# Graph attention on a NeuronCore: the last two node tiles computed from whole adjacency rows instead of gathered neighbour rows

## Chip, cores and metric

The kernel runs on one core of one Trainium2 chip. The metric is the device time of one execution in microseconds (us). Four compute engines matter: TensorE (PE; its weight loads are listed as PEld), VectorE (DVE), ScalarE (ACT) and GpSimd (POOL). SyncE (SP) issues DMAs here, and POOL issues the DMAs that gather or scatter rows by index. POOL in this kernel computes next to nothing: its busy time is the issue of indirect DMAs.

## What is computed

Two graph layers over 4096 nodes of 128 features. The adjacency `adj` is a 4096 x 4096 int32 matrix of zeros and ones, symmetric, with the diagonal set, and about 65 ones in a row. Cut to what matters:

```python
# layer 0: attention with 8 heads over the neighbours
Wh = einsum('nd,hde->hne', x, W);  f1 = Wh . a1;  f2 = Wh . a2      # [8, 4096] each
e = leaky_relu(f1[:, :, None] + f2[:, None, :], 0.2)
att = softmax(where(adj > 0, e, -9e15), axis=-1)
h = elu(einsum('hnm,hmd->hnd', att, Wh))
x = layernorm(x + elu(concat_heads(h) @ W1 + b1)) * gamma + beta
# layer 1: of each node's neighbours every m-th is left out; the rest are sorted
# feature by feature, and the quantiles 0.25, 0.5, 0.75 are averaged
agg = 0.5 * mean_of_quantiles(sorted kept neighbours' x) + 0.5 * x
out = agg @ W.T + b + x
```

Because the attention sums over neighbours first and multiplies by `W` afterwards, a node needs, per head, the weighted sum of its neighbours' x, and only then a product with `W[h]`.

## The kernel before

**Order of the work.** The program has two stages. The first (`gat`, L923) does layer 0 and, mixed into it, builds neighbour lists from the adjacency (`Front`, L302). The second (`sparse`, L1918) gathers, for each of 32 tiles of 128 nodes, the kept neighbours' rows of the new x (`x1_d`) and sorts them on VectorE, with products on TensorE and copies on ScalarE.

**The front.** `Front` reads the adjacency in 32 tiles of 128 rows, grouped into six blocks of 2, 6, 6, 6, 6 and 6 tiles. Each tile's row is read in int32 pieces of 1024 columns (`a_i`, SP's queue), turned to bf16 zeros and ones by ScalarE (`nz`, L380), packed into bit words by TensorE (`ps_words`, L387), and unpacked into lists of node numbers by VectorE (the `MAX8` passes of L191 and L195 among others). Inside a block the 128-row tiles are sorted by degree, so that the last tiles of a block have the longest lists; each node's list, degree and own row go to DRAM as a row of `rows_d`. All this is cut into a list of pieces (`todo`). `advance(n)` runs the next n pieces, and `gat`'s loop calls it between half tiles. What it calls later in the loop is thus what the engines' queues hold later, since each engine takes its instructions in the program's order, apart from priorities set with `issue_after`.

**The table.** `table` (L214) computes, for every node, f1 and f2 of the 8 heads by products with `W·a`, and writes the rows (x, f2, f1) of 144 floats to `xf_d` in DRAM. All neighbour gathers read there.

**The attention loop.** The nodes, in the order of the blocks, make 32 tiles of 128, or 64 half tiles `u` of 64 nodes. A half is four groups of 16 nodes. A partition of a group belongs to one node and one of its eight slots (`SL` = 8). One indirect DMA gathers 128 rows: the next neighbour of each of 16 nodes x 8 slots. So a half needs as many gathers as the sum, over its groups, of a round number: some 30 to 44. Lists are padded with a row that cannot count.

For a half `u` the loop of L1365 and on does this:

- `load(u + 3)` (L1122) issues the gathers of the half three later. They land in `nb` buffers of 18 rows each, of which there are six. A gather waits until the products that used the buffer last are done.
- `rows_sum(u)` multiplies the probabilities with a 0/1 pattern on VectorE (`spread`, L1255), and then TensorE does one f32 128x128 product per gathered set of rows (L1263) into `ps_z`.
- `probabilities(u + 1)` computes the logits and the softmax of the next half on VectorE and ScalarE (L1192 to L1240).
- `collect` (L1278) copies `ps_z` to `zT` on ScalarE.
- Every second tile a generator `combine` is started. One step of it is run per half: products with `W` (L1294), elu, products with `W1`, elu, the layer norm, and an indirect store of the rows of `x1_d` on POOL (L1349).
- `own_row` loads the rows of the tile's own nodes (`me`).

At `u` = 60 the pieces of the front that are left are run, and two POOL gathers fetch the node lists of the first sort tiles. At `u` = 61, behind the last neighbour gather, 24 gathers of x1 rows for the first sort tile are issued (`soon`), which only touch rows of earlier blocks.

The three lines of the neighbour gather's buffers and of its issue, for the names that follow:

```python
rows, used = rowp.tile([P, ROWS, D + H], F32, name="nb"), 0     # 6 buffers, 18 rows each
gather = nc.gpsimd.indirect_dma_start(out=rows[:, used + i, :], in_=xf_d,
    in_offset=bass.IndirectOffsetOnAxis(ap=ids[:, k : k + 1], axis=0))
```

Of the kernel before, what the change touches and what calls it, by code (L numbers as in the profile page):

```python
# [50 lines left out]
P = 128  # L51
# [57 lines left out]

ROWS = 18  # L110
# [103 lines left out]
def table(tc, nc, c, x, w, a1, a2, xf_d, between):  # L214
# [3 lines left out]
    with tc.tile_pool(name="ta", bufs=1) as tp, tc.tile_pool(  # L218
# [33 lines left out]
        for i in range(4):  # L252
            nc.gpsimd.dma_start(
                out=xf_d[1 + i * 1024 : 1 + (i + 1) * 1024, :].rearrange(
                    "(t p) d -> p t d", p=P
                ),
                in_=xf[:, ts(i, 8), :],
            )
# [664 lines left out]
def gat(  # L923
    tc, nc, c, x, adj, xf_d, meta_d, flag_d, w, a1, a2, w1, b1, gamma, beta, x1_d, order, infos, soon
# [26 lines left out]
    with ExitStack() as ctx:  # L951
# [15 lines left out]
        table(tc, nc, c, x, w, a1, a2, xf_d, lambda: advance(2))  # L967
# [56 lines left out]
        def fetch(t):  # L1024
# [34 lines left out]
            info = tp.tile([P, max(BLOCKS), 2], I32, name="info")  # L1059
# [7 lines left out]
        def indices(t):  # L1067

            b = block[t]
            if t in index:  # L1070
                return
            fetch(t)
            ids, first, tops, info, others, ends = fetched[b]
            t0 = START[b]
            for i, (of, k) in enumerate(ends):
                if of == t - t0:
                    to = ids[:, k : k + 1]
                    nc.vector.tensor_tensor(to, to, others[:, i : i + 1], op=ALU.max)
            index[t] = ids, first[t - t0], tops[t - t0], info[:, t - t0, :]
# [3 lines left out]
        def own_row(t):  # L1083
            indices(t)
            if t % TWO == 0:
                me = tp.tile([P, TWO, XF], F32, name="me", bufs=5)
                for j in range(TWO):
                    mes[t + j] = me
# [194 lines left out]
        def combine(t, zT):  # L1283
# [7 lines left out]
            def product(h0):  # L1291
                ps_h = bank().rearrange("p (k n) -> p k n", n=n)
                for k in range(TWO):
                    nc.tensor.matmul(  # L1294
                        ps_h[:, k, :], w_sb[:, h0 + k, :], zT[:, h0 + k, :], start=True, stop=True
                    )
                return ps_h

            pending = []
            for h0 in range(0, H, TWO):  # L1300
                if len(pending) == 2:
                    yield
                    for h, ps_h in pending:
                        elu(nc, zT[:, h : h + TWO, :], ps_h)
# [3 lines left out]
            for h, ps_h in pending:  # L1308
                elu(nc, zT[:, h : h + TWO, :], ps_h)
            ps_y = bank()[:, :n]  # L1310
            for h in range(H):
                nc.tensor.matmul(ps_y, w1_sb[:, h, :], zT[:, h, :], start=h == 0, stop=h == H - 1)
# [47 lines left out]

        stored, ahead = [], []
# [6 lines left out]
        for u in range(2 * NT):  # L1368
            t, half = divmod(u, 2)
            if not half and t + 1 < NT:  # L1370
# [3 lines left out]
            with tc.issue_after(spread):  # L1374
                if u < 2 * START[1]:
                    advance((4, 2, 1, 1)[u])
                elif u < 2 * NT - 4:
                    advance(2 if u in (5, 8) else 1)
# [3 lines left out]
            if u + 3 < 2 * NT:  # L1382
                fetch((u + 3) // 2)
            if u + 1 < 2 * NT:
# [4 lines left out]
            if u + 4 == 2 * NT:  # L1389
# [11 lines left out]
            elif u + 3 < 2 * NT:  # L1401
                held[u + 3] = load(u + 3, after=spread)
            elif u + 3 == 2 * NT:
                with tc.issue_after(gathers[2 * NT - 1][HALF - 1, 0]):
# [10 lines left out]
            with ExitStack() as after:  # L1415
                for ins in behind:
                    after.enter_context(tc.issue_after(ins))
                if u % (2 * TWO) == 0:
                    zT = tp.tile([P, H, TWO * P], F32, name="zT")
                collect(u, ps_z, zT)  # L1420
                for stages in going:
                    next(stages, None)
            if u % (2 * TWO) == 2 * TWO - 1:
                going = going[-1:] + [combine(t - 1, zT)]
# [1089 lines left out]
def gnn(tc, x, adj, w, a1, a2, w1, b1, gamma, beta, lw, lb, out):  # L2514
    nc = tc.nc
    with ExitStack() as ctx:
        dram = ctx.enter_context(tc.tile_pool(name="dram", bufs=1, space=DRAM))
        xf_d = dram.tile([N + 1, XF], F32, name="xf_d")
        x1_d = dram.tile([N + len(PADS), D], F32, name="x1_d")
# [14 lines left out]
            tc, nc, c, x, adj, xf_d, meta_d, flag_d, w, a1, a2, w1, b1, gamma, beta, x1_d,  # L2534
# [43 lines left out]
```

## Time and profile before

| what | value |
|---|---|
| three runs | 8006.99, 8009.91, 8018.21 us; median 8009.91 |
| the profiled execution | 8032.08 us, its span 8030.2 us |
| DVE busy | 5547.1 us, 69% of the span |
| POOL busy | 4358.4 us, 54% |
| ACT busy | 2090.6 us, 26% |
| PE busy, PEld busy | 1431.1 us, 18%; 1107.7 us, 14% |
| DMA | 386.08 MB, 48 GB/s over the span |
| first neighbour gather, last one | 84.6 us, 3424.5 us |
| last store of x1 rows | 3494.5 us |

The page gives busy time by engine, then the span in 40 slices of 201 us with a digit for the busy tenths of each engine, and the costliest groups of instructions. Of its slices these four rows show the two stages:

```profile
PE   4344333333423323310000000000000000000000
...
DVE  4534433433433422258998989999999998997998
...
POOL 5466666656666656665464456545554453454310
PEclk5656655666665656655555555555555555555555
```

The attention stage is the first 17 slices, in which no engine is above six tenths; the sorting stage follows, with VectorE at eight or nine tenths. PEclk is the clock that TensorE was granted, in tenths of full speed. The two groups of indirect gathers are

```profile
L1947 POOL DMA_INDIRECT rows<-x_d,info x2054 | 2054.9, 1000 | 1923.0 <-ACT picked L2047 1304.9
L1122 POOL DMA_INDIRECT nb<-xf_d,ids x2191 | 2105.2, 961 | 1125.2 <-issue 635.0
```

The columns are the line, engine and operation, what it writes and reads, the count, then the busy time and the mean ns of one, then the idle time of the engine just before them and what ended most of it. The first is the sorting stage's, the second the attention's. The last four halves, `u` = 60 to 63, have 36, 37, 39 and 44 gathers.

### The profile page before, as it was taken

The numbers are of one execution on the slowest core, as the hardware profiler recorded it, in microseconds if no ns is written. First come the engines' busy times: TensorE is split into PE (matmuls) and PEld (weight loads), VectorE is DVE, ScalarE is ACT, GpSimd is POOL, SyncE is SP. The second block draws the span as 40 slices with busy tenths as digits, with TensorE's granted clock in tenths as the row PEclk, the third lists the DMA queues.
The fourth block names the chain that finished last, engine by engine and source line by source line (L and its number), as shares of the span: only waits on it lengthen the run. The fifth ranks groups of instructions, "written<-read, shape, count | busy, mean of one in ns | idle before, by whom it ended". The sixth has DMA issues, their size and how long they took to land. (4 is left out here: it accounts for less than half of the span.)

```text
span 8030.2 us, 30780 instructions
## 1 busy us (share of the span) xinstructions
PE 1431.1 (18%) x6349; PEld 1107.7 (14%) x6349; DVE 5547.1 (69%) x8168; ACT 2090.6 (26%) x2423; POOL 4358.4 (54%) x4462
## 2 busy tenths in 40 slices
PE   4344333333423323310000000000000000000000
PEld 2223222322322323310000000000000000000000
DVE  4534433433433422258998989999999998997998
ACT  2111100011000000023343334344443443343333
POOL 5466666656666656665464456545554453454310
PEclk5656655666665656655555555555555555555555
DMA  6432322322322212211111111111111111111100
GB/s 179 93 91 68 76 66 70 69 75 62 57 49 50 57 44 50 49 43 37 29 38 30 31 32 38 36 33 35 36 36 31 33 36 26 30 37 32 26 9 1
DMA packets 279691, 386.08 MB, mean 48 GB/s; under 512 B 189891, under 2 KB 190020, under 8 KB 279476
## 3 DMA queue, kind: packets, MB, share of 16 engines
q0 software_dynamic: 144336, 309.02, 15.9%
q1 hardware_dynamic: 135156, 75.00, 3.6%
q14 instruction: 147, 1.20, 0.1%
q8 instruction: 52, 0.85, 0.0%
HBM read 371.07 MB, written 13.04 MB: 48 GB/s over the span
## 5 line engine op out<-in xcount | busy, mean ns | idle before, releaser
L1992 DVE TENSOR_TENSOR rows<-low,rows 128x1024 f32<-128x1024 f32 (+7 forms) x2118 | 3430.0, 1666 | 248.8 <-ACT low L1985 170.3
L1947 POOL DMA_INDIRECT rows<-x_d,info x2054 | 2054.9, 1000 | 1923.0 <-ACT picked L2047 1304.9
L1122 POOL DMA_INDIRECT nb<-xf_d,ids x2191 | 2105.2, 961 | 1125.2 <-issue 635.0
L1985 ACT COPY low<-rows 128x1024 f32<-128x1024 f32 (+8 forms) x1059 | 1451.9, 1377 | 2110.5 <-DVE rows L1992 1589.4
L1263 PE MATMUL ps_z<-spread,nb 128*128 128x128 f32 x4498 | 801.3, 331 | 1052.6 <-issue 903.7
L1255 DVE TENSOR_TENSOR spread<-e,ps_small 128x1152 f32<-128x1152 f32 (+4 forms) x310 | 338.2, 1115 | 839.0 <-remote 649.7
L1263 PEld LDWEIGHTS ps_z<-spread,nb 128*128 128x128 f32 x4498 | 734.9, 243 | 1131.3 <-issue 999.5
L2054 PE MATMUL low<-sixth_i,picked 128*128 128x128 f32 x300 | 73.0, 425 | 4169.1 <-ACT low L1985 2331.6
L2054 PEld LDWEIGHTS low<-sixth_i,picked 128*128 128x128 f32 x300 | 64.0, 318 | 4178.1 <-ACT low L1985 2336.9
L1992 DVE TENSOR_TENSOR rows<-low_s,rows 128x512 f32<-128x512 f32 (+3 forms) x1056 | 534.2, 540 | 38.9 <-remote 16.0
L1237 ACT ACTIVATE ps_e<-ps_e 128x288 f32<-128x288 f32 (+4 forms) x64 | 24.9, 389 | 2011.2 <-DVE ps_e L1231 1369.8
L1985 ACT COPY low_s<-rows 128x512 f32<-128x512 f32 (+3 forms) x528 | 247.5, 503 | 340.9 <-DVE rows L1992 214.9
L380 ACT ACTIVATE nz<-a_i 128x1024 bf16<-128x1024 int32 x128 | 134.5, 1051 | 673.8 <-remote 266.4
L387 PE MATMUL ps_words<-nz,pows 128*128 128x256 bf16 (+1 forms) x544 | 239.4, 612 | 56.4 <-issue 41.4
L2094 POOL DMA_INDIRECT out<-o,info x32 | 32.0, 1000 | 392.0 <-ACT o L2090 360.1
L1294 PE MATMUL ps_h<-zT,w_ga 128*128 128x256 f32 x256 | 115.3, 613 | 447.2 <-DVE s L1602 208.3
L195 DVE SCALAR_TENSOR_TENSOR key<-key,k 128x256 f32<-128x256 f32 x320 | 151.6, 480 | 44.9 <-remote 10.3
L191 DVE MAX8 k<-key 128x8 f32<-128x256 f32 x352 | 145.0, 420 | 41.7 <-issue 8.1
L1142 DVE TENSOR_TENSOR mine<-me,group 128x64 f32<-128x64 f32 x32 | 6.9, 216 | 223.5 <-remote 144.4
L1192 DVE TENSOR_REDUCE den<-ps_e 128x32 f32<-128x288 f32 (+13 forms) x92 | 31.1, 357 | 187.8 <-ACT ps_e L1237 169.2
L1996 DVE TENSOR_TENSOR rows<-rows 128x256 f32<-128x256 f32 (+7 forms) x259 | 146.9, 574 | 0.0
L1998 DVE TENSOR_TENSOR rows<-rows 128x128 f32<-128x128 f32 (+6 forms) x244 | 142.1, 590 | 3.1 <-remote 2.1
(277 smaller groups left out, 1959.5 us busy)
## 6 DMA issues: line engine op xcount, KB each, us to landing
a_i<-in_adj SPq DMA_DIRECT2D x128, 512.0 KB
nb<-xf_d,ids POOLq DMA_INDIRECT x2191
rows<-x_d,info POOLq DMA_INDIRECT x2054
xf_d<-xf POOLq DMA_DIRECT2D x4, 576.0 KB
soon<-xf_d SPq DMA_DIRECT2D x32, 72.0 KB
me<-rows_d SPq DMA_DIRECT2D x32, 72.0 KB
xf<-in_x POOLq DMA_DIRECT2D x4, 512.0 KB
meta_d<-ids_a SPq DMA_DIRECT2D x5, 324.0 KB
```

Source lines behind the costliest of these rows:

```text
L191: nc.vector.max(out=top, in_=work)
L195: nc.vector.scalar_tensor_tensor(work, work, top[:, 7:8], work, op0=ALU.is_lt, op1=ALU.mult)
L387: nc.tensor.matmul(ps_w[:, :m, ts(i, 2 * part)], self.pows[:, b, :], bits[:, :m, :, b], start=b == 0, stop=b == WBITS - 1,)
L1122: gather = nc.gpsimd.indirect_dma_start(out=rows[:, used + i, :], out_offset=None, in_=xf_d, in_offset=bass.IndirectOffsetOnAxis(ap=ids[:, ...
L1255: last = nc.vector.tensor_tensor(spread[:, :m], e[:, at : at + m, :].unsqueeze(2).to_broadcast(shape), own.unsqueeze(1).unsqueeze(3).to_br ...
L1263: product = nc.tensor.matmul(ps_z[:, g, :], rows[:, k, :D], spread[:, i].rearrange("p j h -> p (j h)"), start=i0 + i == 0, stop=i0 + i == ...
L1947: return nc.gpsimd.indirect_dma_start(out=row, out_offset=None, in_=x1_d, in_offset=bass.IndirectOffsetOnAxis(ap=info[:, col : col + 1], a ...
L1985: nc.scalar.copy(packed, lows)
L1992: done = nc.vector.tensor_tensor(to, packed, highs, op=op)
L1996: nc.vector.tensor_tensor(lows, lows, highs, op=ALU.min)
L1998: nc.vector.tensor_tensor(highs, lows, highs, op=ALU.max)
L2054: product = nc.tensor.matmul(made["ps"], v, to, start=i == 0, stop=i == len(found))
```

## The change

The last two tiles (30 and 31; `LISTED` = 30) leave the loop of halves, which now runs to 60 halves instead of 64. Their attention is computed by a new generator `full()` from the whole rows of the adjacency:

- `table` also writes f2 of all nodes, head by head, to DRAM (`f2_d`, 8 x 4096), by two transposes and two POOL DMAs.
- `full()` first loads x whole, as 32 chunks of 128 nodes (24 into the buffer `soon`, 8 into an `a_i` buffer of the front).
- For each of the two tiles, two indirect DMAs on POOL gather the adjacency rows of its 128 nodes, 2048 columns each, into the front's two `nz` buffers, and VectorE turns them into bf16 masks of 0 and a large negative number, kept in two `a_i` buffers.
- For each head of 8: f2 of all nodes is read to every partition in two DMAs of 1 MB (SP's queue) into the same two `nz` buffers. VectorE adds the mask and takes the maximum in one pass; ScalarE adds f1; VectorE does the leaky relu; ScalarE the exponential, with the sum of a row. That is for two halves of 2048 columns each.
- The probabilities, 128 nodes x 4096, are transposed on TensorE by 32 products with a diagonal matrix that also divides by the sum. ScalarE copies them from PSUM four at a time (into the front's `lists` buffer), and 32 products with the chunks of x accumulate z for the head.
- When all is there, the same `combine` is run for the pair, with `zT` in four buffers of the front.

It uses the front's buffers, and so can begin only when the front's pieces are done. The loop therefore takes two pieces of the front instead of one at every third half from 15 on, so that `todo` is empty after half 41 instead of 50. From then on three steps of `full()` are run per half, behind `collect` and `combine`. There are 34 steps up to the last head's (one for each tile and two for each of its heads), and then `combine`'s. What is left of them at `u` = 57 is run there, ahead of the 24 gathers of `soon`, which moved behind `collect` and which need that buffer. `info` gets three buffers.

The core of the diff:

```diff
+FULLS = 2
+LISTED = NT - FULLS
...
+        f2 = tp.tile([P, H, NT], F32, name="f2_ta")
+        nc.scalar.copy(f2, xf[:, :, D : D + H].rearrange("p t h -> p h t"))
...
+        transpose_all(nc, psum, rows, parts, c["idf"])
+        for i in range(2):
+            nc.gpsimd.dma_start(
+                out=f2_d[ts(i, half), :].rearrange("h (t p) -> (h t) p", p=P),
+                in_=rows[:, ts(i, P)],
             )
...
-                if of == t - t0:
+                if of == t - t0 and t < LISTED:
...
+        def full():
...
+            def wide(dtype):
+                v = fr.tp.tile([P, 2, 2 * quarter], BF, name="nz", bufs=2)
+                return v.rearrange("p m c -> p (m c)").bitcast(dtype)
+
+            for j in range(FULLS):
+                t = LISTED + j
+                own_row(t)
...
+                for q in range(2):
+                    a = wide(I32)
+                    nc.gpsimd.indirect_dma_start(
+                        out=a,
+                        out_offset=None,
+                        in_=adj.rearrange("n (q c) -> (n q) c", q=2),
+                        in_offset=bass.IndirectOffsetOnAxis(ap=rows[:, q : q + 1], axis=0),
+                    )
+                    m = fr.tp.tile([P, quarter], I32, name="a_i", bufs=3).bitcast(BF)
+                    nc.vector.tensor_scalar(m, a, 0.0, -BIG, op0=ALU.is_le, op1=ALU.mult)
+                    masked.append(m)
...
+                yield
+                for h in range(H):
+                    p, tops = [], tp.tile([P, 6], F32, name="tops_f")
+                    for q in range(2):
+                        v = wide(F32)
+                        nc.sync.dma_start(
+                            out=v, in_=f2_d[h, ts(q, N // 2)].partition_broadcast(P)
+                        )
+                        nc.vector.tensor_tensor_reduce(
+                            out=v,
+                            in0=masked[q],
+                            in1=v,
...
+                            op0=ALU.add,
+                            op1=ALU.max,
+                            accum_out=tops[:, q : q + 1],
+                        )
+                        p.append(v)
...
+                    for v in p:
+                        nc.scalar.activation(v, v, AF.Identity, bias=f1, scale=1.0)
+                        nc.vector.scalar_tensor_tensor(v, v, 0.2, v, op0=ALU.mult, op1=ALU.max)
+                    for q, v in enumerate(p):
+                        nc.scalar.activation(
+                            v, v, AF.Exp, bias=less, scale=1.0, accum_out=sums[:, q : q + 1]
+                        )
...
+                    diag = fr.tp.tile([P, NG1], F32, name="key")[:, :P]
+                    nc.vector.tensor_scalar(diag, c["idf"], most, None, op0=ALU.mult)
+                    yield
+                    z = fr.small[:, ts(h % 2, P)]
+                    for k in range(NT // 4):
+                        ps = fr.psum_w.tile([P, 2, NG1], F32, name="ps_words")
+                        ps = ps.rearrange("p m c -> p (m c)")
+                        for i in range(4):
+                            col = (4 * k + i) % (NT // 2)
+                            nc.tensor.matmul(
+                                ps[:, ts(i, P)],
+                                p[(4 * k + i) // (NT // 2)][:, ts(col, P)],
+                                diag,
+                                start=True,
+                                stop=True,
+                            )
+                        pT = fr.tp.tile([P, max(BLOCKS), C1], F32, name="lists")
+                        pT = pT.rearrange("p t c -> p (t c)")[:, : 4 * P]
+                        nc.scalar.copy(pT, ps)
+                        for i in range(4):
+                            m = 4 * k + i
+                            chunk = xs[:, m, :] if m < NT * 3 // 4 else rest[:, m - NT * 3 // 4, :]
+                            nc.tensor.matmul(
+                                z, chunk, pT[:, ts(i, P)], start=m == 0, stop=m == NT - 1
+                            )
+                    nc.scalar.copy(zT(h - h % TWO)[:, h % TWO, ts(j, P)], z)
+                    yield
+            for _ in combine(LISTED, zT):
+                yield
...
-        for u in range(2 * NT):
+        halves_of = 2 * LISTED
+        rest = None
+        for u in range(halves_of):
...
-                elif u < 2 * NT - 4:
-                    advance(2 if u in (5, 8) else 1)
+                elif todo:
+                    advance(2 if u in (5, 8) or u > 12 and u % 3 == 0 else 1)
...
+            if u + 3 == halves_of:
+                for _ in rest:
+                    pass
+                with tc.issue_after(gathers[halves_of - 1][HALF - 1, 0]):
                     for i in range(HIGH[0] - SOON):
...
+            if rest is None and not todo:
+                rest = full()
+            for _ in range(3 if rest is not None else 0):
+                next(rest, None)
+        for _ in rest:
+            pass
```

## The prediction

> **What bounds the kernel now.** I read the busy table by stage first, then GpSimd's (POOL's) timeline in the attention stage, then what its gathers wait for, then TensorE and VectorE beside them. By stage (stretch, its length, then busy us and count of PE, PEld, DVE, ACT, POOL; granted clock, DMA share, GB/s):
>
> ```profile
> 3000.00:3250.00 250.00, 82.02 (x384) 69.41 (x384) 60.52 (x159) 15.08 (x29) 165.15 (x175) 0.60 0.21 49
> 4000.00:5000.00 1000.00, 35.75 (x128) 29.21 (x128) 924.07 (x897) 390.78 (x418) 544.97 (x516) 0.50 0.13 34
> ```
>
> The first is attention (84 to 3495 us), the second the second layer's sorting. Sorting is VectorE's, at 92%; the change does not touch it. In attention POOL is the fullest, at 66%, and that understates it, as its timeline shows:
>
> ```profile
> 3190.49 0.94 POOL L1122 DMA_INDIRECT nb<-xf_d,ids  x1 [0.30 <-issue]
> 3191.74 0.94 POOL L1122 DMA_INDIRECT nb<-xf_d,ids  x1 [0.30 <-issue]
> 3199.27 0.94 POOL L1122 DMA_INDIRECT nb<-xf_d,ids  x1 [6.58 <-PE ps_z L1263]
> 3200.51 0.94 POOL L1122 DMA_INDIRECT nb<-xf_d,ids  x1 [0.30 <-issue]
> ...
> 3424.47 0.94 POOL L1122 DMA_INDIRECT nb<-xf_d,ids  x1 [0.30 <-issue]
> ```
>
> A gather costs 0.94 us and 0.30 before the next: one per 1.25 us. About once per half tile POOL stops, because a row buffer is not free yet. Over the 2191 gathers, the idle time before them:
>
> ```profile
>   issue: 635.0, 2082
>   PE ps_z L1263: 253.3, 23
>   remote: 216.0, 43
> ```
>
> So the stage is 2191 x 1.25 = 2740 us of issue and some 470 us of stops for the products of `rows_sum`, three halves back. Those products are late for a reason that this change meets head on:
>
> ```profile
> 2410.39 0.37 PE L1263 MATMUL ps_z<-spread,nb 128*128 128x128 f32 x1 [2.43 <-issue]
> 2410.40 0.21 DVE L1160 STREAM_TRANSPOSE den_t<-den 128x32 f32<-128x32 f32 x1 [1.64 <-remote]
> 2411.79 0.29 PEld L1263 LDWEIGHTS ps_z<-spread,nb 128*128 128x128 f32 x1 [2.51 <-issue]
> 2412.49 0.37 PE L1263 MATMUL ps_z<-spread,nb 128*128 128x128 f32 x1 [1.73 <-issue]
> 2412.50 0.19 DVE L1164 TENSOR_REDUCE den_b<-den_t 128x4 f32<-128x32 f32 x1 [0.91 <-issue]
> ...
> 2429.99 1.23 PE L1263 MATMUL ps_z<-spread,nb 128*128 128x128 f32 x5 [1.03 <-issue]
> ```
>
> I call this the crawl: TensorE and VectorE each take about one instruction per 1.4 us, on one common beat, waiting for nothing that is shown. Setting its 408 slow products against POOL's timeline, they lie some 17 us or more into an unbroken run of gathers, or within 7 us after it; at 2424 POOL stops and by 2430 the products run at full speed again. Halves with short runs (products at 2300 to 2309 and 2363 to 2372) have none.
>
> **The change, part by part.** The profiled execution's span is 8030 us, 8032 with what lies around it, 22 us over the median of the runs, 8010; differences are worked out inside the profile and put on 8010.
>
> *Removed.* Halves 60 to 63 with 36 + 37 + 39 + 44 = 156 gathers. On POOL they fill 3199.3 to 3425.4, 226 us with their stops. The two node-list gathers (1.25 each) and two of the four stores (1.3 each) inside stay: -221. What follows the last gather (store at 3494.5, 70 us on) is the same chain for half 59: nothing.
>
> *f2 rows at the start.* Two more POOL DMAs behind the four `xf_d` stores (3.61 us together), a copy and two transposes (four take 1.09 us, their copy 0.59). POOL then idles 10.64 us before `w_ga`, waiting for DVE: hidden. Without that cover 5 us.
>
> *Front pieces sooner.* The same 50-odd pieces, now two at every third half from 13 on, so that the front ends at half 41, not 50. The sum of DVE work is unchanged. Halves in which a heavy piece delays DVE show stops of 19 to 31 us (before 1006.6, 1150.4, 1638.0, 2875.8); two in one half may make one stop longer and spare another. I take 0, bounds -30 and +30.
>
> *Two tiles from full rows.* Three steps per half from half 41; 16 heads (8 per tile) at two steps each, 1.5 heads per half, over 10.7 halves. Per head, from the nearest rows:
>
> ```profile
> L1992 DVE TENSOR_TENSOR rows<-low,rows 128x2048 f32<-128x2048 f32 x654 | 1469.7, 2280 | 65.7 <-ACT low L1985 58.0 <-issue 4.3
> L1985 ACT COPY low<-rows 128x2048 f32<-128x2048 f32 x327 | 610.1, 1869 | 733.7 <-DVE rows L1992 595.8 <-issue 127.3 <-DMA rows<-x_d,info 9.4
> L1278 ACT COPY zT<-ps_z 128x512 f32<-128x512 f32 x64 | 37.7, 589 | 284.0 <-remote 158.9 <-PE ps_z L1263 119.3 <-issue 5.8
> ```
>
> - DVE: four passes of 2048, 4 x 2.28 = 9.1, and seven small ones at 0.2: 10.5 us.
> - ACT: four of 2048, 4 x 1.87 = 7.5, eight copies of 512, 4.7, one of 128: 12.4 us.
> - PE: 32 products with the diagonal and 32 with x, all f32 128x128. Such a product shows as two records, and 62 records took 8.99 us: 128 x 0.145 = 18.6 us. The bf16 products of L387 took 0.243 us each at 10 to 40 us, where the granted clock was 0.88, and 0.466 in attention; by that ratio a busier PE would need 9.7. I take 18, since waits for ACT break it up.
> - DMA: two reads of 1 MB. The core moved 272 GB/s at 10 to 40 us and 178 at 40 to 80: 3.9 to 5.9 us each, with about 2 to land: 8.
>
> None is over 47 us per half at 1.5 heads (PE 28 + 10 for `rows_sum`, DVE 16 + some 20). But both halves of a row live in the two `nz` buffers, and the next head's f2 can land there only after TensorE has read them. So heads are serial: products to the last read 16, DMA 8, masked maximum 2.3, ACT 1.9, leaky 2.3, exp 1.9, scale and handoffs 1.5: 34 us. In the built order of VectorE the next head's first maximum stands ahead of `spread` of every second half, and a whole head between a half's last softmax instruction (L1240 of before) and it. What queues behind that wait is `spread`, behind it `rows_sum`, behind it the row buffers, and so POOL. Three heads then pace two halves: 3 x 34 = 102 and some 10 of `spread` and products that nothing covers, 56 us per half. Before, halves 41 to 53 took (2912 - 2252) / 13 = 50.8.
>
> Next the crawl. POOL's runs stay 28 to 44 gathers long, 35 to 55 us, so some 20 to 30 us of each half fall under it, and a head has 256 PE records where a half of `rows_sum` had 140. At about one per 1.2 us it all but stands there. The loss per half lies between 0 (PE would have waited for f2 or DVE anyway, as it does for half of a head) and 28 (it always needs PE); I take 19, nearer the upper end, because freed buffers start POOL just when the next head's products come.
>
> VectorE's long passes may slow gathers: beside two-input passes at 2030.71 one took 1.97 us instead of 0.95. With 64 passes that is at most 64 us of issue, most of it in POOL's own stops: I take 0. The Trainium skill speaks against the change here: "GPSIMD Engine Reference", section "Key points", has POOL share its SBUF interfaces with VectorE, with contention for instructions that have two SBUF inputs. All 64 passes have two; by the rule the 64 us would stand, by the row only part.
>
> Adjacency rows: four POOL DMAs and two maskings of 2.3 per tile, x into `soon`: about 15 us that the first head of each tile waits, bounds 5 and 30.
>
> *Sum.* A half of 56 + 19 = 75 is 24 over before, x 10.7 = +258; -221 + 258 + 15 = +52: 8062, rounded up to 8070 for the two combine steps that come on top. The change breaks even at 70 us per half.
>
> **Rivals.**
> - *Heads serial, crawl not felt* (PE waits for f2 while POOL runs): 56 to 68 per half, -221 + 15 + 56..184, so 7860 to 7988; about 7890. For it: crawl spares long ACT and DVE instructions. Against: it strikes every engine but POOL in the trace.
> - *POOL still paces*: at the clock of 0.88 the head's products take 9.7, the chain 26, two halves 88, under POOL's 2 x 47. Then only 221 less 5 to 20: 7800. The Trainium skill's "TensorE: Matmul & The Clock Gate", section "What's actually happening", says the array is throttled by default and sustained activity releases it; the trace agrees with 0.50 idle and 0.88 busy. By that rule this rival would gain weight, by the attention rows (0.60) not.
> - *Slower by far*: crawl takes 28 and f2 reads share the DMA engines (now 0.25 busy) with gathers, 90 or more per half from half 41 on: -221 + 30 + 420 = 8240. It decides above 70.
>
> **How the numbers follow.** Forecast (70 to 88 per half) 0.48, 8000 to 8200; crawl not felt 0.29; POOL paces 0.13; slower by far 0.10. The likeliest gives 8070, with its own range 8010 to 8200. The range, 7830 to 8230, takes in "crawl not felt" whole; it leaves out "POOL still paces" (0.13) and the far end of "slower by far" (some 0.07), 2 in 10 together. Within 0.2% of 8010 (16 us, what a measurement can tell) lies a thin slice of the first two: 0.06. Faster 0.38, slower 0.56.
>
> **What would show it.** 2035 gathers and their end near 3250 to 3300 if I am right, below 3230 if the gain holds; halves from 41 on of about 75 us against 48 before 41 and after 54; POOL stops of 20 us and more there, ended by PE; f32 products of the heads at one per 1.4 us while POOL runs. The sorting stage should last the same 4530 us. Products at full speed beside long gather runs would refute the crawl, and halves near 48 the serial heads.

## The result, and the profile after

The changed kernel took 8216.28 us (median of 4 runs, 8213.94 to 8236.33) against 8013.65 (4 runs): a ratio of 1.0259, interval 1.0241 to 1.0277. It is slower, as forecast, but by 203 us, where the forecast of 8070 stood for 60 over its 8010. The time is inside the stated range, but outside the forecast's own (8010 to 8200).

The attention stage is 212 us longer in the profiled execution. Where they come from is found by counting POOL's neighbour gathers off in both traces (a half has 28 to 44) and taking the start of each half's first gather:

| stretch | before, us | after, us | difference |
|---|---|---|---|
| to the start of half 44 (no head's products yet) | 2382.3 | 2423.7 | +41.4 |
| halves 44 to 55 (the heads' halves) | 624.1 | 999.4 | +375.3 |
| halves 56 to 59 (of after, to the end of the last gather) | 192.9 | 194.2 | +1.3 |
| halves 60 to 63, to the end of the last gather | 226.1 | none | -226.1 |
| end of the last gather to the last store of x1 | 69.1 | 89.5 | +20.4 |

The sum is +212.3. The sorting stage that follows lasted 4509.5 us against 4535.7. Part of the 41.4 may be chance: in `after_again` and `after_b`, two more traces of the changed kernel on other chips, half 44 begins at 2401.6 and at 2447.7 us. Halves 44 to 55 take 83.3 us in the mean in the changed kernel, and 83.2 and 84.2 in those two. The two stretches that the prediction shows of the kernel before, in the busy table by stage of the changed kernel (same columns):

```profile
3000.00:3250.00 250.00, 120.22 (x804) 114.67 (x804) 75.46 (x130) 62.92 (x79) 80.72 (x84) 0.71 0.21 63
4000.00:5000.00 1000.00, 39.69 (x153) 32.96 (x151) 910.97 (x905) 386.29 (x420) 530.11 (x505) 0.51 0.13 33
```

In attention POOL's busy time has halved, from 165 to 81 us in 250: it isn't issuing more slowly, it is standing still. What its gathers waited for, from the source view of the gather's line (L1141 now, L1122 before):

```profile
  PE ps_z L1282: 656.7, 31
  issue: 590.0, 1934
  remote: 141.8, 28
```

The stops for the products of `rows_sum` rose from 253 to 657 us. "issue", in which POOL waited for nothing that the profile shows, fell with the number of gathers. So the row buffers come free later, because TensorE gets to `rows_sum` later. Why it does is in the timeline of ScalarE and TensorE, first for a head (number 5 of tile 30, counted from 0) whose products lie under a run of gathers:

```profile
2760.40 1.16 PE L1491 MATMUL ps_small<-lists,soon 128*128 128x128 f32 x8 [0.79 <-issue]
2766.82 0.59 ACT L1487 COPY lists<-ps_words 128x512 f32<-128x512 f32 x1 [6.47 <-remote]
2767.46 2.08 PE L1491 MATMUL ps_small<-lists,soon 128*128 128x128 f32 x8 [5.90 <-issue]
...
2769.76 3.19 PE L1478 MATMUL ps_words<-key,nz 128*128 128x128 f32 x14
...
2800.53 0.59 ACT L1487 COPY lists<-ps_words 128x512 f32<-128x512 f32 x1 [33.12 <-remote]
```

and for the next head, whose products fall in POOL's stop of 2794.6 to 2853.3:

```profile
2831.85 1.87 PEld L1478 LDWEIGHTS ps_words<-key,nz 128*128 128x128 f32 x16
2833.11 0.59 ACT L1487 COPY lists<-ps_words 128x512 f32<-128x512 f32 x1 [2.20 <-PE ps_words L1478]
...
2836.78 0.59 ACT L1487 COPY lists<-ps_words 128x512 f32<-128x512 f32 x1 [2.20 <-PE ps_words L1478]
2837.67 0.59 ACT L1487 COPY lists<-ps_words 128x512 f32<-128x512 f32 x1 [0.31 <-PE ps_words L1478]
...
2843.80 0.27 ACT L1494 COPY k<-ps_small 128x128 f32<-128x128 f32 x1 [1.25 <-PE ps_small L1491]
```

In the second, a copy follows its transposing products within a microsecond of their end. In the first, the products of the line before it are through by 2773, and the copy that needs them begins at 2800.5, six microseconds after POOL's last gather of the run, with "remote" as the reason: a wait that the profile can name no releaser for. That is what the prediction called the crawl, in the form it takes in a head. From its first product to its last copy a head took 19 to 22 us in POOL's stops (5 of 16 heads, one of them only in part) and 28 to 83 under gathers; heads were 31 to 32 us apart where one lay in a stop, and 52 to 102 otherwise (61.5 in the mean of all).

### The profile page after: what moved, and what is told of

Its sections match the earlier page's. It is cut to its first block, busy times and chain, and to the rows that moved or that the text cites. A ratio compares the mean times of both kernels' runs of the same rounds, so it can differ in the third digit from the quotient of the medians.

```text
span 8216.3 us, 34499 instructions
## 1 busy us (share of the span) xinstructions
PE 1638.4 (20%) x8077; PEld 1316.3 (16%) x8077; DVE 5657.7 (69%) x8266; ACT 2294.0 (28%) x2657; POOL 4259.0 (52%) x4312
## 5 line engine op out<-in xcount | busy, mean ns | idle before, releaser
L1141 POOL DMA_INDIRECT nb<-xf_d,ids x2035 | 1997.0, 981 | 1409.1 <-PE ps_z L1282 656.7
L1282 PE MATMUL ps_z<-spread,nb 128*128 128x128 f32 x4180 | 709.9, 326 | 811.8 <-issue 592.7
L1274 DVE TENSOR_TENSOR spread<-e,ps_small 128x1024 f32<-128x1024 f32 (+4 forms) x284 | 313.7, 1129 | 718.0 <-remote 551.7
L1282 PEld LDWEIGHTS ps_z<-spread,nb 128*128 128x128 f32 x4180 | 656.7, 238 | 876.2 <-issue 727.6
L1441 DVE CUSTOM_DVE_ANT_0 nz<-a_i,nz 128x2048 f32<-128x2048 bf16 x32 | 73.3, 2289 | 422.5 <-DMA nz<-f_d 295.2
L1487 ACT COPY lists<-ps_words 128x512 f32<-128x512 f32 x128 | 73.9, 585 | 552.7 <-remote 393.2
L1491 PE MATMUL ps_small<-lists,soon 128*128 128x128 f32 x768 | 133.1, 336 | 325.2 <-ACT lists L1487 226.4
L1478 PE MATMUL ps_words<-key,nz 128*128 128x128 f32 x1024 | 157.0, 315 | 116.5 <-DVE key L1470 67.8
L1491 PEld LDWEIGHTS ps_small<-lists,soon 128*128 128x128 f32 x768 | 120.3, 242 | 334.2 <-ACT lists L1487 231.3
L1478 PEld LDWEIGHTS ps_words<-key,nz 128*128 128x128 f32 x1024 | 149.0, 229 | 120.5 <-ACT nz L1464 69.8
```

Of the source, the lines that this page charges most:

```text
L1274: last = nc.vector.tensor_tensor(spread[:, :m], e[:, at : at + m, :].unsqueeze(2).to_broadcast(shape), own.unsqueeze(1).unsqueeze(3).to_br ...
L1282: product = nc.tensor.matmul(ps_z[:, g, :], rows[:, k, :D], spread[:, i].rearrange("p j h -> p (j h)"), start=i0 + i == 0, stop=i0 + i == ...
L1478: nc.tensor.matmul(ps[:, ts(i, P)], p[(4 * k + i) // (NT // 2)][:, ts(col, P)], diag, start=True, stop=True,)
L1491: nc.tensor.matmul(z, chunk, pT[:, ts(i, P)], start=m == 0, stop=m == NT - 1)
```

## The experiments

The runs fell on several chips, and these are of two kinds. On three (and in the runs of the result) the kernel before takes 8013 to 8051 us, on two 7302 to 7304. The crawl is seen on the first kind alone, called chips with the crawl from here on. Each ratio is against the kernel before on the same chip.

| kernel | before there | ratio | interval |
|---|---|---|---|
| pace_only | 7304 | 1.0006 | 0.9997 to 1.0016 |
| pace_again | 8026 | 0.9986 | 0.9967 to 1.0004 |
| heads_alone | 7304 | 1.0382 | 1.0361 to 1.0402 |
| few_products | 7304 | 0.9883 | 0.9863 to 0.9903 |
| few_again | 8051 | 0.9857 | 0.9842 to 0.9873 |
| pauses12 | 7304 | 0.9987 | 0.9978 to 0.9997 |
| after_again (unaltered) | 8017 | 1.0230 | 1.0215 to 1.0245 |
| after_b (unaltered) | 8051 | 1.0288 | 1.0273 to 1.0303 |
| two_steps | 8017 | 1.0173 | 1.0158 to 1.0189 |
| one_head | 8017 | 1.0167 | 1.0150 to 1.0185 |
| paused | 8051 | 1.0149 | 1.0134 to 1.0165 |
| paused_one | 8051 | 1.0082 | 1.0067 to 1.0098 |
| split | 8026 | 1.0384 | 1.0345 to 1.0422 |
| bf16 | 8026 | 1.0060 | 1.0040 to 1.0081 |
| bf16_two | 8026 | 1.0044 | 1.0023 to 1.0065 |
| bf16_paused | 7302 | 1.0162 | 1.0146 to 1.0179 |
| bf16_two_paused | 7302 | 1.0115 | 1.0098 to 1.0132 |
| bf16_two_paused_b | 8047 | 0.9965 | 0.9950 to 0.9979 |

**The front's pace, and one kernel on two kinds of chip.** `pace_only` and `pace_again` are one kernel: no tile from full rows.

```diff
-FULLS = 2
+FULLS = 0
...
-            if rest is None and not todo:
-                rest = full()
...
```

> All 32 tiles come from gathered rows again; only the front's pieces keep the changed kernel's pace (two at every third half), and f2 is still written. In the changed kernel halves 0 to 43 ended 41 us later than before, although no head had begun before half 43. If the sooner front itself costs that, this kernel lies some 41 us over the kernel before, less what halves 42 to 50 save since they have no pieces left (up to 30): 8020 to 8055. If I was right to cost it at nothing: within 30 us of 8013, and no more than 10 from it if pieces only move.

> All 32 tiles from gathered rows, the front's pieces at the changed kernel's pace, as in pace_only, but wanted on a chip with the crawl, where the changed kernel's halves 0 to 43 (with no head yet) ended 41 us late. If the sooner pieces cost that by themselves: ratio 1.002 to 1.005 (41 us less what halves 42 to 50 save). If they only move work: 0.999 to 1.001. Without the crawl 1.0006 was measured.

On neither chip does the pace cost anything that can be measured. With the crawl the halves run 39.8 us behind the kernel before at half 44, much as in the changed kernel (41.4), and 11 behind at half 60. That looks like time spent early and given back, but the trace of the kernel before is of another session, and the changed kernel's own traces differ by 46 us at this point. The pair shows the two kinds of chip at one program. The groups of the gathers and of `rows_sum`'s products on the page without the crawl:

```profile
L1141 POOL DMA_INDIRECT nb<-xf_d,ids x2191 | 2111.4, 964 | 679.5 <-issue 643.1
L1282 PE MATMUL ps_z<-spread,nb 128*128 128x128 f32 x4498 | 576.6, 295 | 189.0 <-DVE spread L1274 188.9
L2133 DVE TENSOR_TENSOR rows<-low,rows 128x1024 f32<-128x1024 f32 (+7 forms) x2118 | 3437.7, 1675 | 68.3 <-ACT low L2126 43.1
```

and with it:

```profile
L1141 POOL DMA_INDIRECT nb<-xf_d,ids x2191 | 2104.2, 960 | 1138.2 <-issue 620.5
L1282 PE MATMUL ps_z<-spread,nb 128*128 128x128 f32 x4498 | 802.7, 332 | 1092.5 <-issue 848.5
L2133 DVE TENSOR_TENSOR rows<-low,rows 128x1024 f32<-128x1024 f32 (+7 forms) x2118 | 3428.6, 1664 | 228.3 <-ACT low L2126 125.3
```

The gathers and VectorE's passes take as long on both. What differs is idle time: TensorE's "issue", 848 us where the other page has 188.9 of 189.0 us as waits for `spread`, POOL's stops (5.9 us for products there against 268), and the hand-overs of the sort. In the trace without the crawl POOL's runs are hundreds of us long, and not one of the 4498 product records of `rows_sum` has more than 0.7 us of idle time before it that the profile names no releaser for; with the crawl 415 have. So all that the prediction called the crawl was seen on one kind of chip only. Each chip served one session (one of them two, 27 minutes apart), so whether the crawl belongs to the chip or to its state at the time isn't shown.

**The heads without gathers beside them.** No step of `full()` runs in the loop; all are run where the drain stands.

```diff
-            for _ in range(3 if rest is not None else 0):
+            for _ in range(0 if rest is not None else 0):
```

> No step of the heads runs in the loop of halves; all 16 run one after the other when the row gathers have been issued up to the last buffers, so POOL is silent beside them. Theory 'turns' (a head is 31 us long when POOL is silent, and every longer head of the changed kernel is longer only because its instructions fall under a run of gathers): heads 31 us apart, 16 x 31 + 20 = 516 us in all; gathers end near 3240, the last x1 store some 3240 + 516 = 3760, total 8260 to 8300. Rival 'long heads' (the 61.5 us per head of the changed kernel are the heads' own chain of reads, passes and products): 16 x 61.5 = 984 us, total near 8740.

This ran on a chip without the crawl. Heads are 31 us apart: 14 of the 15 spacings lie between 28.2 and 32.7, and the first head of tile 31, with its adjacency rows, is 43 behind its predecessor. With the crawl, too, heads are 31 to 32 us apart where one lies in a stop of POOL's. So the serial chain is 31 us, and what is over that in the changed kernel isn't the heads' own. The ratio shows what 16 x 31 us cost when nothing hides them.

**The unaltered kernel elsewhere, and fewer heads per half.** `two_steps` and `one_head`:

```diff
-            for _ in range(3 if rest is not None else 0):
+            for _ in range(2 if rest is not None else 0):
...
-                    advance(2 if u in (5, 8) or u > 12 and u % 3 == 0 else 1)
+                    advance(2 if u in (5, 8) or u > 12 and u % 2 == 0 else 1)
```

(the second hunk in `one_head` alone)

> The changed kernel itself, unaltered, beside the kernel before on the chip that these four kernels share. The four kernels run so far were on a chip where the kernel before takes 7304 us, not 8013; in their traces no instruction crawls and POOL never stops for a product outside the heads' halves. If the crawl under long gather runs is what made the change cost 203 us, then on a chip without it the changed kernel is near the kernel before: halves with heads take some 56 us (3 x 34 + 10 over two), about 15 more than POOL's 41 there, so -203 + 12 x 15 + 25 for the start of each tile: 7270 to 7330. If the heads' length alone did it, it is slower by some 200 there too: 7500. On a chip with the crawl: 8205 to 8235 against 8005 to 8020.

> The changed kernel unaltered once more, beside the three that follow, to tell what chip they share. On a chip where instructions crawl under long gather runs (kernel before near 8015): ratio 1.022 to 1.027. On one where they don't (kernel before near 7304): near 7285, ratio 0.995 to 1.000, by the kernel with the one-column copies, which differs by 39 copies of 0.35 us.

> Two steps of the heads per half instead of three, so one head per half from half 41 on, and what is left of them at half 57 behind the loads of the last half. Without the crawl: a head of 31 us lies in a half of 42 to 58 us of gathers beside 12 us of sums, so POOL paces again but for its slower gathers under VectorE's passes (some 2 us per head) and the heads left over (2 to 3 heads, 31 us each, at the end): 7304 - 203 + 16 x 3 + 80 = 7230. With the crawl: each head still takes its 31 us from POOL, only in other places: 8200 to 8260, no better than three steps. 'Long heads' (61 us each whatever POOL does): a half of 73 us, 17 of them, on either chip no gain over three steps.

> As two_steps, and the front takes two pieces at every second half from 14 on instead of every third, so that the heads begin some three halves sooner and are through before half 57. Without the crawl: no heads left over at the end, 7304 - 203 + 16 x 3 + 10 = 7160. With the crawl: the pieces in earlier halves cost what they cost, 8190 to 8260.

All four ran on chips with the crawl. With one head per half, halves 45 to 49 take 69 to 80 us and the heads are 52 to 104 apart (but for the last of `two_steps`, 36): each still takes 20 us and more from POOL. The gain over three steps is 0.6%, and an earlier start adds nothing that can be told from none (the intervals overlap).

**POOL's pauses.** `pauses12` was meant as a pause on POOL, by one copy of a column behind every 12th gather. It was none: POOL went on 0.35 us later, so on its chip it is the changed kernel with 39 small copies. (In this edit and the next the constants are written out.)

```diff
                     gathers[u][g, i] = gather.ins
+                    since[0] += 1
+                    if 44 <= u < 58 and since[0] % 12 == 0:
+                        nc.gpsimd.tensor_copy(landed, rows[:, used + i, :1])
```

> The changed kernel, with a copy of one column on POOL after every 12th row gather in halves 44 to 57, which waits until that gather has landed; nothing else. 'Turns', with a crawl that only begins 15 to 25 us into an unbroken run of gathers: runs of 12 gathers are 15 us, each pause some 3 us, so no product crawls, POOL needs 34 x 1.25 + 3 x 3 = 52 us per half, heads and sums 1.5 x 31 + 12 = 58, and a half takes 60 instead of 82: 8215 - 12 x 22 = 7950. If a pause of 3 us doesn't end the crawl: halves of 85 to 90 and 8250 to 8310. 'Long heads': pauses only add time, 8215 to 8330, with heads still 50 to 100 us apart.

It tells what the change is worth without the crawl: nothing to speak of, 7294 us against 7304. Halves 44 to 48 take 55.3, 51.7, 54.0, 56.0 and 58.8 us, and POOL paces them: of these 276 us it stopped 4.6 for the products of `rows_sum` (the source view of the gather's line, from 2053.5 to 2329.3 us):

```profile
  issue: 47.3, 162
  PE ps_z L1287: 4.6, 2
```

The halves are longer than the 44 us of `pace_only` because gathers are slower: 49 in the whole run, beside VectorE's long passes for the heads, took 1.6 to 3.1 us, against 0.94 for most. Halves 49 to 52 are another matter. They take 67.4, 110.9, 65.3 and 64.2 us, and POOL stops 86 us in them for products. They follow the start of tile 31, whose adjacency rows are gathered by POOL behind the neighbour gathers in its queue; VectorE stands until they land, and `spread` stands behind VectorE's pass. Without the crawl and in the changed kernel:

```profile
2370.11 1.23 DVE L1430 TENSOR_SCALAR a_i<-nz 128x2048 bf16<-128x2048 int32 x1 [38.32 <-DMA nz<-in_adj,rows_f]
2901.95 1.23 DVE L1425 TENSOR_SCALAR a_i<-nz 128x2048 bf16<-128x2048 int32 x1 [37.87 <-DMA nz<-in_adj,rows_f]
```

Without the crawl heads are mostly 30 to 40 us apart, and their copies never wait for "remote". This is the source view of that copy's line, on the chip without the crawl:

```profile
  PE ps_words L1483: 169.5, 109
  PE ps_small L1496: 27.6, 2
```

and of the same copy in the changed kernel:

```profile
  remote: 393.2, 23
  PE ps_words L1478: 147.6, 76
  issue: 11.8, 6
```

`paused` makes real pauses, `paused_one` adds them to `one_head` (from half 40, behind every 14th gather):

```diff
+                    if 44 <= u < 58 and since[0] % 12 == 0:
+                        for _ in range(16):
+                            held_back.append(
+                                nc.gpsimd.tensor_copy(idle, rows[:, used + i, :1]).ins
+                            )
```

(and the next gather is issued behind the last copy)

> The changed kernel with 16 copies of one column on POOL behind every 12th gather of halves 44 to 57, nothing else: POOL issues no gather for some 5.6 us. With the crawl, if it is a backlog that a run of gathers builds up in 15 to 25 us and that needs 5 to 7 us to drain: no run is longer than 15 us, no product crawls, POOL needs 47 + 3 x 5.6 = 64 us per half and the heads and sums 58, a half takes 66 instead of 82: 8000. If pauses of 5.6 us don't help: 64 + what the heads take from POOL, 85 to 100 per half: 8230 to 8400. Without the crawl POOL's pauses alone count: 41 + 17 = 58 to 62 per half against 55 to 65: 7300 to 7350.

> One head per half and the front faster, as in one_head, with the pauses behind every 14th gather from half 40 on. With the crawl, if pauses end it: POOL 47 + 2.4 x 5.6 = 60 per half instead of 70 over 16 halves: 8147 - 160 = 7990. If they don't: 8230 and over. Without the crawl: POOL paces with its pauses, 41 + 13 = 55 per half over 17 halves: 7280 to 7320.

Taking time from POOL made the kernel faster, by 116 us against the unaltered kernel on that chip, and from 1.0167 to 1.0082 against `one_head`, each on its own chip. A pause on the timeline of `paused`, and then, from the source view, the waits of its heads' copies:

```profile
2550.89 3.85 POOL L1157 COPY idle<-nb 128x1 f32<-128x1 f32 x16 [1.64 <-DMA nb<-xf_d,ids]
```

```profile
  PE ps_words L1489: 170.6, 77
  remote: 103.7, 19
  issue: 41.6, 7
```

With runs of 12 gathers "remote" falls from 396 us in the unaltered kernel on that chip to 104, POOL's stops for products from 696 to 337, and a head's products and copies from 28 to 83 us to 19 to 34, but for one of 70. That shows the cause on such a chip: POOL's gathers slow the heads. Whether it is the length of a run or the number of gathers per us isn't told apart by it, since a pause lowers both; the count of slow products in the last section speaks for the length. Both gains are about half of what I expected: halves 44 to 49 came down from 85 to 75 us in the mean, not to 66.

**How much of a head pays.** `few_products` and `few_again` (one kernel) leave out 7 of 8 of a head's products and copies.

```diff
-                    for k in range(NT // 4):
+                    for k in range(1):
```

> Leaves out 7 of 8 of a head's products with the diagonal and with x and of the copies between them, so that x1 of the last two tiles comes from 512 of 4096 neighbours. Reads of f2, maxima, leaky relu and exponentials stay. 'Turns' (everything of a head, VectorE's and ScalarE's passes too, has to run while POOL pauses): a head of 31 - 17 = 14 us in 1.5 heads per half still adds some 20 us to a half, 8215 - 12 x (31 - 20) = some 8080. 'Products alone crawl' (passes of 2 us don't feel it, one beat each): halves near 52, 8215 - 370 = 7845 to 7900. 'Long heads': the chain of a head less its products is 61 - 20 or more, 1.5 of them 62 per half, so about 8060 to 8100 too; the spacing of heads (31 - 17 = 14 when POOL is silent) tells it from 'turns'.

> Leaves out 7 of 8 of a head's products and of the copies between them, as before. Without the crawl 7216 as measured, ratio 0.988. With the crawl: if a head pays for all that it does (turns with POOL), 14 of its 31 us remain, 1.5 of them per half: 8200 - 12 x (31 - 14 x 1.5 x 31 / 46) = about 8000, near the kernel before. If its products alone pay, halves near 52 and 7850. If products matter no more than the rest, 8150 and over.

On a chip with the crawl this takes 343 us off the changed kernel (8279 to 7937), without it some 78 (7294 to 7217, against `pauses12`). Set against the kernel before, the changed kernel is 228 us slower with the crawl and 10 faster without; with an eighth of the products it is 115 and 87 us faster. So the head's products, with the copies between them, carry nearly all of the crawl's price; the long passes of VectorE and ScalarE carry little. Neither of my figures for the chip with the crawl (8000 and 7850) was right; 7937 lies between them.

**What is paid per instruction?** `split` makes each product with the diagonal twice, 64 columns wide. `bf16` holds the exponentials, the diagonal and x in bf16 for the products; `bf16_two` adds two steps per half.

```diff
+                            for w in range(2):
+                                nc.tensor.matmul(
+                                    ps[:, ts(2 * i + w, P // 2)],
...
+                                    diag[:, ts(w, P // 2)],
```

```diff
+            xs = soon[:, : NT * 3 // 4, :].rearrange("p t d -> p (t d)").bitcast(BF)
...
+                            v.bitcast(BF)[:, : N // 2],
...
+                    diag = fr.tp.tile([P, NG1], F32, name="key").bitcast(BF)[:, :P]
```

> Each of a head's 32 products with the diagonal is made as two of 64 columns: 64 more PE instructions of the same data and the same columns, 32 products more per head. If the crawl is paid per instruction: a head's products take longer by 32 of 256 to 64 of 256 records, 5 to 15 us per head of those under gathers, ratio 1.030 to 1.045. If it is paid per column or per time: no change, 1.022 to 1.029. Without the crawl: up to 3 us per head, 1.000 to 1.005.

> The exponentials, the diagonal and x are in bf16 for the heads' products (and x is loaded as bf16 by POOL's queue); as many products and copies, but a bf16 product is one record, not two, and shorter. Everything else as in the changed kernel. If the crawl is paid per PE instruction: 128 records per head instead of 256; alone a head's products fall from 20 us to some 10 and under gathers from 40..80 to some 30; a half takes some 68 instead of 82: ratio 1.022 - 12 x 14 / 8015 = 1.001 to 1.006. If PE's records don't matter and the copies of ScalarE (as many as before) set the crawl's price: 1.018 to 1.027. Without the crawl: heads of 22 us hide under the gathers, 0.985 to 0.990.

> bf16 with two steps per half instead of three. With the crawl, two steps were worth 0.6% (1.023 to 1.0173): 0.995 to 1.000 if records count, and then the first version under the kernel before on such a chip that computes all; 1.015 if they don't. Without the crawl 0.980 to 0.987.

Both moved as expected, and yet `split` doesn't settle it. Its group on the page:

```profile
L1479 PE MATMUL ps_words<-key,nz 128*128 128x64 f32 x2048 | 324.6, 326 | 137.4 <-DVE key L1470 73.3 <-DVE den_t L1179 22.9 <-issue 22.8
```

A product of 64 columns took 326 ns a record, one of 128 took 315 in the changed kernel, so the split products are 168 us more of TensorE, and the copies' "remote" stayed at 404 us. In `bf16` the heads' products fell from 327 us of TensorE to 137, the copies' "remote" only from 393 to 302. Both results fit a price on a head's length as well; that each instruction pays a price of its own isn't shown.

**A version under the kernel before.** bf16 with pauses, and two steps per half in the second:

> bf16 products, and POOL pauses (12 copies of one column, some 4.2 us) behind every 12th gather of halves 44 to 57. With the crawl, pauses took 1.4% off the changed kernel in f32, where a head had 256 records; with 128 they can save half of that: ratio 0.998 to 1.002. If the records that are left are no longer what POOL stops for, the pauses only cost, 39 x 4.2 = 164 us of which POOL's stops hide most: 1.006 to 1.015. Without the crawl 0.985 to 0.995.

> bf16 products, two steps per half, and pauses of 10 copies (3.5 us) behind every 14th gather of halves 44 to 58. With the crawl: 1.0044 less some 0.5%: 0.997 to 1.001. If pauses only cost: 1.006 to 1.012. Without the crawl 0.980 to 0.990.

> The same kernel once more, wanted on a chip with the crawl: the run before fell on one without it (kernel before 7302 us), where pauses can only cost (1.0115). With the crawl, if unbroken gather runs are what slows TensorE: 0.997 to 1.001, under bf16_two's 1.0044. If pauses only cost there too: 1.008 to 1.015. Without the crawl 1.0115 again.

The first two fell on a chip without the crawl, where the pauses have nothing to win; no bf16 kernel without pauses ran there, so their price alone isn't measured. On one with it `bf16_two_paused_b` is the only kernel with the whole computation that beats the kernel before, by 0.35%; its halves 44 to 58 take 59.6 us in the mean. It isn't better on both kinds of chip: the same kernel is 1.15% slower without the crawl. `bf16_two` on a chip without the crawl wasn't tried.

## Why the prediction was right in kind and wrong in size

In the profiles the attention stage grew by 212 us, where the sum had +52. Of the 160 us between, 102 lie in the heads' halves (375 against 258 + 15), 41 ahead of them, 20 behind the last gather and 1 in halves 56 to 59; the removed halves gave 5 more than the sum had. The sorting stage then gave 26 back, of the size by which its length differs among the other traces with the crawl (4507 to 4533 us).

- *Removed gathers, -221.* Right: -226.1 for halves 60 to 63. What follows the last gather was put at nothing and came out 20.4 longer.
- *f2 rows at the start, 0.* Right: the first neighbour gather issues at 84.7 us, at 84.6 before.
- *Front sooner, 0.* Right as a sum, by the `pace` kernels. Of the 41 us of the early halves the share that is the change's own isn't known, since the same program varies by 46 us there.
- *Heads serial, 34 us each and 56 per half.* The chain is right: 31 us alone. The 56 was met by luck where there is no crawl: halves 44 to 48 took 52 to 59 us, but it was POOL that paced them, slowed by VectorE's passes, and not the heads. Over all twelve halves it was 59.3.
- *The crawl, 19 per half.* The step that failed: "The loss per half lies between 0 (PE would have waited for f2 or DVE anyway, as it does for half of a head) and 28 (it always needs PE); I take 19". The heads' halves took 83.3 us in the mean, 27 over 56, the upper end, and 24 over the 59.3 of the chip without the crawl. I had reasoned that a part of the loss would fall where TensorE waits anyway. The trace shows the opposite order: POOL restarts when `rows_sum` frees its buffers, the next head's softmax runs at the start of the new run, at full speed, and its products begin 2 to 20 us into the run and so reach into its slow part. Eleven of 16 heads met it.
- *10.7 halves.* The second term that was too small. It was 12: the heads' steps reach to half 55. At 31 us over before each, that is +375 instead of +258.
- *Adjacency rows, 15, bounds 5 and 30.* Too low. VectorE stood 38 us for those of tile 31, with the crawl and without, because the sum had priced the gathers and the maskings and not their place in POOL's queue. Half 50, just behind, was the longest of all: 135.6 us, and 110.9 without the crawl. This lies inside the +375.
- *VectorE's passes on the gathers, 0.* Too low. Without the crawl the mean gather rose from 964 ns (`pace_only`) to 1005 (`pauses12`), 2035 x 0.041 = 83 us; with it from 961 to 981, 41 us. The rule of the Trainium skill's "GPSIMD Engine Reference", "Key points", that VectorE's instructions with two SBUF inputs contend with POOL, which shares its SBUF interfaces, points the way the measurement went, and the estimate of 64 us was the better figure.
- *The rivals.* "Crawl not felt" is near what happens on chips that have no crawl; the gain is 0.1% and not the 1.5% that I gave, since there a half of the kernel before takes 46 us (44 to 51 of `pace_only`), not 51, and one of `pauses12` 65. "POOL still paces" fails with the crawl, and without it holds for halves 44 to 48 and not for 49 to 52. Its price rested on a misreading: the 0.243 and 0.466 us of L387 are products of 128 columns and of 256, so their ratio says nothing of the clock. The head's products took 17 us of TensorE at a granted clock of 0.80 (2050 to 2550 us of `pauses12`), not 9.7. The clock did rise under the heads, from 0.60 to 0.71 with the crawl, and from 0.63 (`pace_only`) to 0.80 without.

## What to carry to other kernels

Before an engine's spare time is given new work, ask when in the bottleneck's cycle that work will fall, not only how much there is: here the new products arrived in exactly the part of POOL's run in which TensorE and its hand-overs stand almost still. A bottleneck that slows its neighbours can be worth pausing. And a cost that the trace shows as idle time without a releaser should be taken at its upper bound until a run has placed it; whether it is the kernel's or the chip's shows only when one program is run on several.

## What the runs showed of the hardware

That two chips of one type differ by 9.7% at one program (7307 and 8017 us for the `pace` kernel), with nearly equal durations of gathers and passes and most of the difference in idle time, was not expected. The slow stretches begin some 15 us into an unbroken run of POOL's and grow denser with its age. In the trace of the kernel before, 1 of the 1437 product records of `rows_sum` that begin in the first 10 us of a run is slow (more than 0.7 us idle before it, no releaser), 93 of 939 from 15 to 25 us, and 135 of 301 from 30 to 45. They outlast the run by some 7 us, and it isn't data that is then still under way. The table by stretch of the kernel before, around the end of a run, whose last instruction is a store of x1 rows at 2424.0 us (columns as above, with the DMA share and GB/s last):

```profile
2424.00:2426.00 2.00, 0.06 (x1) 0.29 (x1) 0.43 (x1) 0.00 (x0) 0.98 (x1) 0.50 0.20 66
2426.00:2428.00 2.00, 0.37 (x1) 0.11 (x1) 0.00 (x0) 0.00 (x0) 0.00 (x0) 0.50 0.00 0
2428.00:2430.00 2.00, 0.38 (x2) 0.47 (x3) 0.00 (x0) 0.00 (x0) 0.00 (x0) 0.50 0.00 0
2430.00:2432.00 2.00, 1.22 (x5) 0.93 (x4) 0.00 (x0) 0.00 (x0) 1.40 (x2) 0.50 0.05 13
```

From 2426 to 2430 POOL is idle and the DMA engines move nothing, and TensorE still takes one product every 1 to 2 us. What the engines wait for then, and why it isn't there in the sessions on the two other chips, stays open.
